# SiLU written as tanh in a two-layer kernel: activation in the exponentials' table, product on VectorE

## The chip, the cores and the metric

The kernel runs on one core of a Trainium2 chip. The metric is the device time of one execution in microseconds (us); a time given for a kernel is the median of several executions. The engines are called as the profile calls them: PE (TensorE, matrix multiplications), PEld (PE's weight loads), DVE (VectorE), ACT (ScalarE, activations), POOL (GpSimd) and SP (the queue that issues most DMAs). PSUM is the memory that PE writes to, in eight banks; SBUF is the working memory.

## The reference, cut to what matters

Two layers, each a gated residual: `x = x + s * g`, where `s` comes from one branch and `g = silu(f)` from another, both computed from the layer-normalised `x` (2 sequences of 2048 tokens, 256 channels).

```python
x = L0_attn_x
xn = _layernorm(x, axis=-1)
s = _L0_attn_ref(xn, ...)          # linear attention (elu features), then @ W_out
g = _silu(_L0_ffn_ref(xn, ...))    # softmax attention block, then a mixture of 8 experts
x = x + s * g
xn = _layernorm(x, axis=-1)
s = _L1_attn_ref(xn, ...)          # causal softmax attention, 16 heads, then @ Wo
g = _silu(_L1_ffn_ref(xn, ...))    # one quantised linear map plus a low-rank one
x = x + s * g
```

`silu(v) = v / (1 + exp(-v))`, which is the same as `0.5 * v * (1 + tanh(v / 2))`.

## The kernel before, in words

Tokens lie in 32 tiles of 128 (16 per sequence); `xr` holds all of them in SBUF. The work has three stages, one after the other.

1. **Layer 0's attentions** (from 0 to about 1440 us). The softmax attention of the expert branch, with the linear branch `s` worked in between. The linear branch's result is copied from PSUM by ACT (line 1199) and stored to the DRAM tensor `s_dram`.
2. **The experts** (to about 1931 us). Two halves of eight experts; for each, PE multiplies by W1 (L1380), ACT applies Gelu (L1381), PE multiplies by W2 (L1386), DVE adds the bias (L1389). Within it `early_mix` finishes layer 0 for the first four tiles: POOL gathers the expert rows (L1337), DVE weighs and adds them (L1344 to L1346), ACT applies Silu (L1348), DVE multiplies by `s` and adds `x` (L1349, L1350).
3. **Layer 1's attention** (to the end). Per sequence and group of four heads, pass A finds each query's maximum (PE L554, DVE L573 or, on the diagonal, L567), pass B computes scores again (PE L587, L1585, L520), ACT takes the exponentials into `pt` (L599), POOL adds up pairs of key tiles in `ps` (L1597 to L1602), PE multiplies by the values and sums (L1620, L1631), DVE collects (L1635, L1637), and `finish` projects with `wo` (PE L1676), multiplies by the gate (DVE L1680) and adds to `xr` (POOL L1686).

Between these run two side jobs of stage 3 that contain a SiLU:

- **`mix`** finishes layer 0 for the other 28 tiles, two tiles (one buffer pair `gx`, `xs`; there are two of each) at a time: four gathers by POOL (L1459), weighing by ACT (L1468), two additions by DVE (L1473, L1474), Silu by ACT (L1439), then times `s` and plus `x` (L1481, L1482), on DVE for the first sequence and on POOL for the second, and the statistics of the next layer norm (L491 on) for every four tiles. For the second sequence `mix` is called with four tiles: both pairs' Silus are then one step, so that they are together. Those four calls come at units 24, 40, 56 and 72 of the attention's loop.
- **`gate`** computes layer 1's `g` for four tiles: PE L1698, L1713, L1714 into two PSUM banks, then one ACT step with both Silus (L1720), which reads PSUM and writes `gs`, then DMAs to the DRAM tensor `g_dram`; `finish` loads it again.

Stages 1 and 3 are ordered by hand: every piece of work is a step `S(strand, engine, cost, function, reads, writes)`, and `Plan.run` searches, with these costs in us, for the order in which steps are issued; each engine then executes its steps strictly in that order. A changed cost or step can therefore change the order of everything after it. Stage 2 is ordered by the Tile scheduler.

ACT evaluates its functions from a table that must be loaded (ACT_TABLE_LOAD in the profile). Exp, Gelu and Silu are loaded separately here; the compiler puts a load wherever the next function is not in the table that is there.

## Time and profile before

| | us |
|---|---|
| five runs | 3439.91, 3442.41, 3443.70, 3433.20, 3444.74 |
| median | 3442.41 |
| the profiled execution, its own time | 3440.51 |
| the profiled execution, span from first to last instruction | 3438.7 |
| PE busy | 3317.3 (96%) |
| DVE busy | 2077.0 (60%) |
| ACT busy | 1669.3 (49%) |
| POOL busy | 1664.5 (48%) |

A page or an answer of the trace names a group of instructions by the line of the kernel, the engine, the operation, what it writes and reads, how often it ran, its busy time and the mean of one; then the time that the engine sat idle just before and who released it. "PE banks L1631 <- POOL ps L1602" reads: PE's instruction of line 1631 waited for POOL's of line 1602. Time in a window counts from the first instruction.

### The profile page before, as it was taken

Reading aid. Unit: us, or ns where it says so; the run is one execution under the profiler, and the core shown is the slowest. Engines: PE = TensorE matmul, PEld = TensorE weight load, DVE = VectorE, ACT = ScalarE, POOL = GpSimd, SP = SyncE. Lnnn points to the kernel's source line nnn. Section 1 sums busy time; section 2 is a strip of 40 time slices with the busy share of each in tenths; the row PEclk is TensorE's granted clock in tenths of the full one; section 3 lists DMA queues with packets and bytes.
Section 4 is the critical chain, followed back from the end, with each engine's and each line's share of the span. In section 5 each row is a group of like instructions: output and inputs, shape, how many; then the busy total and the mean of one; then the engine's idle time right before and its main releaser. Section 6 shows DMA issues by size and latency. Waiting matters only on the chain.

```text
span 3438.7 us, 84330 instructions
## 1 busy us (share of the span) xinstructions
PE 3317.3 (96%) x35894; PEld 2327.5 (68%) x35894; DVE 2077.0 (60%) x4066; ACT 1669.3 (49%) x3330; POOL 1664.5 (48%) x2239
## 2 busy tenths in 40 slices
PE   6999999999999999799899999999999999999998
PEld 5667777776777777566566566666676666766675
DVE  4767676777676768511111377676666566666674
ACT  3565555555555555411221364555455545454554
POOL 5452322324232223300100268898786567787876
PEclk7999999999999999899999999999999999999999
DMA  5000000000000010233333211110000100000000
GB/s 182 2 2 2 8 8 8 17 20 32 8 8 5 8 39 25 96 106 108 117 115 97 69 49 50 52 49 12 17 16 26 38 28 14 22 14 19 14 26 23
DMA packets 99514, 133.21 MB, mean 39 GB/s; under 512 B 9395, under 2 KB 76671, under 8 KB 99138
## 3 DMA queue, kind: packets, MB, share of 16 engines
q1 hardware_dynamic: 92994, 113.95, 10.3%
q0 software_dynamic: 6144, 13.88, 1.3%
q8 instruction: 281, 4.60, 0.5%
q14 instruction: 95, 0.78, 0.1%
HBM read 92.96 MB, written 37.75 MB: 38 GB/s over the span
## 4 chain that ended last, share of the span: by engine, by line
PE 78%; POOL 12%; DVE 4%; issue 3%; ACT 2%; DMA 1%; SPq 0%; POOLq 0%; DVEq 0%; ACTq 0%
PE banks L554 14%; PE banks L587 13%; PE banks L838 7%; PE s L1386 6%; PE s L1380 6%; PE banks L1620 5%; PE banks L520 4%; PE banks L1527 3%; POOL ps L1601 3%; PE banks L768 3%; POOL ps L1602 2%; POOL ps L1597 2%; PE banks L1585 2%; DVE mx L573 2%; PE banks L1100 2%
## 5 line engine op out<-in xcount | busy, mean ns | idle before, releaser
L599 ACT ACTIVATE pt<-banks 128x512 f32<-128x512 f32 (+1 forms) x2304 | 1164.0, 575 | 712.2 <-PE banks L520 209.3
L573 DVE TENSOR_REDUCE mx<-banks 128x2 f32<-128x1024 f32 (+3 forms) x1024 | 1120.9, 1122 | 336.2 <-PE banks L587 140.0
L554 PE MATMUL banks<-carried,carried 32*128 32x512 f32 (+3 forms) x5120 | 1233.2, 559 | 13.4 <-DVE mx L573 6.1
L587 PE MATMUL banks<-carried,carried 32*128 32x256 f32 (+1 forms) x9216 | 1237.0, 387 | 2.1 <-DVE mx L573 1.6
L587 PEld LDWEIGHTS banks<-carried,carried 32*128 32x128 f32 x9216 | 924.0, 185 | 35.0 <-DVE mx L573 5.2
L554 PEld LDWEIGHTS banks<-carried,carried 32*128 32x128 f32 x5120 | 482.6, 185 | 208.2 <-issue 112.8
L1597 POOL TENSOR_TENSOR ps<-pt 128x1024 f32<-128x1024 f32 (+1 forms) x159 | 343.2, 2158 | 144.4 <-ACT pt L599 118.3
L1601 POOL TENSOR_TENSOR ps<-ps,pt 128x1024 f32<-128x1024 f32 x127 | 300.8, 2369 | 68.2 <-ACT pt L599 63.7
L775 POOL TENSOR_TENSOR ra<-raw,rope 128x128 f32<-128x128 f32 x128 | 60.2, 470 | 557.5 <-ACT raw L787 479.9
L1585 PE MATMUL banks<-mh,ones_h 3*128 3x512 bf16 (+1 forms) x1152 | 292.3, 368 | 0.1
L567 DVE CUSTOM_DVE_ANT_0 banks<-banks,causal 128x384 f32<-128x384 f32 (+3 forms) x512 | 242.1, 513 | 58.4 <-PE banks L554 50.9
L1620 PE MATMUL banks<-pt,vt 128*32 128x256 f32 (+1 forms) x4608 | 270.8, 373 | 2.7 <-ACT pt L599 2.6
L1602 POOL TENSOR_TENSOR ps<-ps,pt 128x1024 f32<-128x1024 f32 (+1 forms) x127 | 267.9, 2109 | 10.0
L838 PE MATMUL banks<-pt,vt 128*32 128x256 f32 (+1 forms) x4608 | 268.2, 371 | 2.0 <-DVE mx L573 1.4
L1389 DVE TENSOR_TENSOR ye<-s,b 128x256 f32<-128x256 f32 x64 | 27.2, 425 | 386.3 <-PE s L1386 386.3
L1381 ACT ACTIVATE hm<-s,b1c 128x512 f32<-128x512 f32 x128 | 87.8, 687 | 351.9 <-PE s L1380 351.9
L1386 PE MATMUL s<-carried,hm 128*128 128x256 f32 x1024 | 226.6, 382 | 7.7 <-ACT hm L1381 7.7
L1380 PE MATMUL s<-xt,carried 128*128 128x512 f32 x512 | 225.9, 599 | 7.1 <-DVE xt L1322 7.0
L1620 PEld LDWEIGHTS banks<-pt,vt 128*32 128x32 f32 x4608 | 134.2, 110 | 140.7 <-ACT pt L599 42.0
L1386 PEld LDWEIGHTS s<-carried,hm 128*128 128x128 f32 x1024 | 196.4, 192 | 42.1 <-ACT hm L1381 8.1
L520 PEld LDWEIGHTS <-ident_h 32*128 32x128 bf16 x4096 | 201.5, 93 | 30.7 <-issue 15.4
L838 PEld LDWEIGHTS banks<-pt,vt 128*32 128x32 f32 x4608 | 133.3, 109 | 117.3 <-issue 14.9
(273 smaller groups left out, 4165.4 us busy)
## 6 DMA issues: line engine op xcount, KB each, us to landing
carried<-in_L_ffn_W_dram SPq DMA_DIRECT2D x32, 1024.0 KB, 5.9
gl<-g_dram SPq DMA_DIRECT2D x64, 256.0 KB, 2.8
slots_in<-zero SPq DMA_DIRECT2D x8, 1024.0 KB, 11.1
xe<-slots_in SPq DMA_DIRECT2D x16, 512.0 KB, 7.6
slots_out<-ye SPq DMA_DIRECT2D x16, 512.0 KB, 6.9
s_dram<-lo SPq DMA_DIRECT2D x16, 256.0 KB, 2.0
hn<-in_L_attn_x_dram SPq DMA_DIRECT2D x16, 256.0 KB, 2.8
g_dram<-gs SPq DMA_DIRECT2D x16, 256.0 KB, 2.2
```

The costliest lines, as they stand in the source:

```text
L520: nc.tensor.matmul(out, ident_h[r, q], mask[r, q], start=False, stop=q == 3)
L554: nc.tensor.matmul(s.t[:, x, :w], g.qt.t[r, t * P : (t + 1) * P], g.kt.t[r, 512 * k : 512 * k + w], start=True, stop=not (diagonal and cau ...
L573: S("A", "DVE", t_dve(2 * w), lambda: nc.vector.tensor_reduce(mx.t[:, t % 2, i : i + 2, k], s.t[:, :, :w], AX.X, ALU.max), r=[(s, 0), (s, ...
L587: nc.tensor.matmul(s.t[:, at], g.kt.t[r, kj * P : (kj + 1) * P], g.qt.t[r, QC * c + q0 : QC * (c + 1)], start=n == 0, stop=n == 1 and not ...
L599: S("B", "ACT", t_act(w), lambda: nc.scalar.activation(pt.t[:, j, :w], s.t[:, :w], AF.Exp, scale=0.25), r=[s], w=[(pt, j)])
L838: nc.tensor.matmul(av.t[32 * j : 32 * j + 32, q0:QC], vts[G.vn][:, kj, j], pt.t[:, j, at], start=n == 0, stop=n == len(tiles) - 1,)
L1380: nc.tensor.matmul(ps, w1[:, k, f * P : (f + 1) * P], xt[:, k], start=k == 0, stop=k == 1)
L1386: nc.tensor.matmul(ps[:, :D], hm[:, f, s * P : (s + 1) * P], w2[:, f], start=f == 0, stop=f == FF // P - 1)
L1585: return lambda: nc.tensor.matmul(s.t[:, :w_], ones_h[r], G.mh[c].t[r, 512 - w_ :], start=False, stop=last)
L1597: nc.gpsimd.tensor_tensor(ps.t[:, :, q0:], pt.t[:, :, same], pt.t[:, :, odd], ALU.add)
L1601: nc.gpsimd.tensor_tensor(ps.t, ps.t, pt.t[:, :, even], ALU.add)
L1620: nc.tensor.matmul(av.t[32 * j : 32 * j + 32, q0:QC], G.vt.t[:, kj, j], pt.t[:, j, at], start=n == 0, stop=False)
```

## The change

Silu is replaced by Tanh with the input scaled by 0.5, followed by one `scalar_tensor_tensor` on DVE that computes `(tanh + 1) * v`. The result is twice the SiLU, so a factor of 0.5 is put elsewhere: in layer 0 on the linear branch's result when it is copied from PSUM, in layer 1 on the output weights `wo`, once, by POOL. With that, `gate`'s step for two Silus becomes four steps (one Tanh and one product for each pair), the step costs given to the planner change, and the second sequence's `mix` is called eight times with two tiles (at units 24, 32, ..., 80) instead of four times with four.

```diff
-            S("lin", "ACT", 0.59, lambda: nc.scalar.copy(so.t.rearrange("p n d -> p (n d)"), sp.t), r=[sp], w=[so])
+            S("lin", "ACT", 0.59, lambda: nc.scalar.mul(so.t.rearrange("p n d -> p (n d)"), sp.t, 0.5), r=[sp], w=[so])
...
-            nc.scalar.activation(gx[:, 0], gx[:, 0], AF.Silu)
+            nc.scalar.activation(gx[:, 1], gx[:, 0], AF.Tanh, scale=0.5)
+            nc.vector.scalar_tensor_tensor(gx[:, 0], gx[:, 1], 1.0, gx[:, 0], ALU.add, ALU.mult)
...
                     load_l1()
+                    nc.gpsimd.tensor_scalar_mul(wo, wo, 0.5)
...
-                    nc.scalar.activation(gx.t[:, 0], gx.t[:, 0], AF.Silu)
+                    nc.scalar.activation(gx.t[:, 1], gx.t[:, 0], AF.Tanh, scale=0.5)
...
-            S("mix", "ACT", 1.4 + 0.6 * len(both), silus, r=got, w=got)
+            S("mix", "ACT", 0.6 * len(both), silus, r=got, w=got)
...
+            S("mix", "DVE", 1.0, lambda: nc.vector.scalar_tensor_tensor(
+                gx.t[:, 0], gx.t[:, 1], 1.0, gx.t[:, 0], ALU.add, ALU.mult
+            ), r=[gx], w=[gx])
...
-            def silu():
-                for py, gl in pairs:
-                    nc.scalar.activation(gl.t.rearrange("p n d -> p (n d)"), py.t, AF.Silu)
-
-            S("gate", "ACT", 4.0, silu, r=[py for py, _ in pairs], w=[gl for _, gl in pairs])
+            def silu(py, gl):
+                nc.scalar.activation(gl.t.rearrange("p n d -> p (n d)"), py.t, AF.Tanh, scale=0.5)
+
+            def times(py, gl):
+                g_ = gl.t.rearrange("p n d -> p (n d)")
+                nc.vector.scalar_tensor_tensor(g_, g_, 1.0, py.t, ALU.add, ALU.mult)
+
+            for py, gl in pairs:
+                S("gate", "ACT", 0.6, lambda py=py, gl=gl: silu(py, gl), r=[py], w=[gl])
+                S("gate", "DVE", 0.7, lambda py=py, gl=gl: times(py, gl), r=[py, gl], w=[gl])
...
-        others = [(24 + 16 * n, lambda n0=NT + 4 * n: mix(n0, 4)) for n in range(NT // 4)]
+        others = [(24 + 8 * n, lambda n0=NT + 2 * n: mix(n0)) for n in range(NT // 2)]
```

## The prediction

> **What bounds the kernel now.** I read the page first: the table of engines, the slices, the chain.

> ```profile
> PE 3317.3 (96%) x35894; PEld 2327.5 (68%) x35894; DVE 2077.0 (60%) x4066; ACT 1669.3 (49%) x3330; POOL 1664.5 (48%) x2239
> ...
> PE   6999999999999999799899999999999999999998
> ...
> POOL 5452322324232223300100268898786567787876
> PE 78%; POOL 12%; DVE 4%; issue 3%; ACT 2%; DMA 1%; SPq 0%; POOLq 0%; DVEq 0%; ACTq 0%
> ```

> PE sets the end: it is busy in every slice but the first and two near the experts, and it holds 78% of the chain that ended last. ACT holds 2% of that chain, though it is busy for 49% of the span. So a microsecond taken from ACT is worth one only where PE was waiting for it. POOL holds 12%, and is at eight to nine tenths in slices 24 to 27, which is where the second sequence's `mix` runs.

> Next the groups of ACT's instructions, for what the change takes away:

> ```profile
> L599 ACT ACT_TABLE_LOAD x15 | 19.2, 1283 | 2.8 <-PE banks L1714 1.4 <-PE banks L1585 1.2
> ...
> L1439 ACT ACT_TABLE_LOAD x9 | 11.5, 1283 | 0.2
> ...
> L1720 ACT ACT_TABLE_LOAD x6 | 7.7, 1283 | 0.1
> ...
> L1348 ACT ACT_TABLE_LOAD x1 | 1.3, 1283 | 0.0
> ```

> Thirty loads of 1283 ns lie in stage 3, from 1942.9 to 2788.5 us: 38.5 us of ACT. Then who held PE up in stage 3 (window 1930 to 3439, the waits of PE alone; who waited for whom, total, times, longest):

> ```profile
> PE banks L1631 <- POOL ps L1602: 11.6, 10, 2.4
> PE banks L1571 <- POOL mpad L1567: 6.5, 14, 1.6
> PE banks L554 <- DVE mx L573: 2.8, 14, 0.4
> PE banks L1620 <- ACT pt L599: 2.6, 7, 1.3
> PE banks L372 <- ACT hn L1501: 2.3, 4, 1.2
> ```

> All waits for ACT in that answer add up to 10.5 us (2.6 for `pt` and 2.3 for `hn` above; 1.4, 1.2, 1.1, 1.1 and 0.8 in rows not shown), those for POOL to 18.4 (11.6, 6.5, 0.3), those for DVE to 8.7. In 1500 us, ACT costs PE 10.5 us whatever it does. That is the ceiling for the direct gain, not 38.5.

> **The change part by part.** The sum starts from the profiled execution's 3440.5 us, 1.9 below the median of the five runs (3442.4); I add the 1.9 at the end.

> *Loads.* In the changed program as built, ACT's order has 3 loads instead of 34: Exp at the start, Gelu at the experts, Exp at layer 1. Tanh needs none of its own, beside Gelu either. Two terms follow.

> (a) The early Silu, among the experts. Here the timeline shows ACT on the path:

> ```profile
> 1711.99 1.28 ACT L1381 ACT_TABLE_LOAD   x1
> ...
> 1713.29 0.69 ACT L1381 ACTIVATE hm<-s,b1c 128x512 f32<-128x512 f32 x1
> ...
> 1714.03 12.48 PE L1386 MATMUL s<-carried,hm 128*128 128x256 f32 x44 [7.67 <-ACT hm L1381]
> ```

> PE stood 7.67 us, because ACT, in its order, waited for the gathered rows of `early_g` before it could do the last Gelu. The load before the Silu (1701.07) lies inside that wait of 8.57 us and is worth nothing; the load after it is in the path: **-1.3 us**. The new product on DVE (128x1024; the neighbouring L1349 took 1.22) comes after Tanh and delays only early_mix's own end, and the bias addition L1389 by under 0.5 us, which PE's other banks cover. The wait of 7.67 stays otherwise: the place in the order is the same, after 71 Gelus.

> (b) Stage 3. I went through PE's stops after each load: 0.68 us at 1964.8 (`xt` behind a load and three exponentials), 0.53 at 1976.1, 0.44 at 2002.9, 0.64 at 2099.5, 1.32 at 2633.8, each with a load just ahead of the `pt` or `xt` that PE waited for. Sum 3.6: **-3.6 us**. The other 25 loads are hidden by PE's own work, as ACT idles 362.6 us before L599 in stage 3. Bounds: 0 (something else is late next) to -10.5 (all waits for ACT).

> [...]

> (c) *Smaller portions of `mix`.* Total work on POOL stays (32 gathers, 16 operations of 1.27 us for the second sequence), but it comes in eight portions instead of four. One call of four tiles gives POOL 8 gathers of 1.0 with 0.3 between them and 4 operations, some 15 us at once, while its sums for the attention (L1597 to L1602, 2.4 us each for a full tile) go on. From 2080 to 2360, PE's waits for POOL are 9.5 us (5.7 for `ps` L1602, 3.5 for `mpad`, 0.3). With half portions the backlog halves, the average load of POOL (89% there) does not. Between 0 and -9.5 I take a third: **-3.0 us**.

> (d) *The new product of `mix` on DVE.* 14 instructions, 6 for the first sequence and 8 for the second, each reading two operands from SBUF. The undisturbed price is that of the same form in L1084, 680 to 694 ns. But the rows that stand right beside it say more:

> ```profile
> L1473 DVE TENSOR_TENSOR gx<-gx,xr x14: 674/692/3500, 1941.7 to 2321.4; 128x512 f32<-128x512 f32 x14
> ```

> ```profile
> 2081.03 3.50 DVE L1473 TENSOR_TENSOR gx<-gx,xr 128x512 f32<-128x512 f32 x1
> ```

> At the same time POOL ran a gather and then the 2.36 us of L1597; DVE's instruction ended after POOL's. For the 16 executions of L1473 and L1474 from 2080 to 2360 the means are 1.61 and 1.39 us, 0.81 above 0.69. So the eight new ones bring 8 x 0.81 = 6.5 us of stall on DVE beside 14 x 0.69 = 9.7 of work. DVE's reduction L573 frees the banks into which PE writes; it is 64 to 77% busy in the stretches there. In the stretch after the 3.50 us PE stopped 1.05 us for L573, so a stall is passed on in part. Between 0 and +6.5 I take half: **+3.3 us**. POOL pays too: its additions took 2.69 to 2.82 instead of 2.36 us when they met these; that is within (c)'s bounds.

> [...]

> (e) *The product of `gate`.* 16 instructions that read one operand from PSUM. L1680 has that shape and takes 673 to 690 ns in all 64 executions, never more, so 11 us on a DVE that is 58% busy from 2600 to 2800. It holds a PSUM bank for 0.7 us longer, plus DVE's queue; on the other hand ACT no longer waits between the two Silus in one step (20.7 us of idle time before L1720 for PE), so exponentials can go between. Between -1.5 and +3: **+0.5 us**.

> (f) *Nothing:* L1199 as a multiplication costs what L1154 does, 597 instead of 585 ns, 16 times, on an ACT that waits for PE there; stage 1's order is unchanged. The scaling of `wo` is one POOL operation of 128x1024, about twice L1599's 0.64 us, placed where POOL then idles 242 us. The stores of `g` (SP) come one by one, and are needed tens of us later. In the start of stage 3 (1931 to 2080) the chain from gather to projection loses loads and gains a product of 0.7 for each pair; in the new order the second pair's Tanh stands behind the first gate's, so I count no gain beyond (b) there.

> Sum: -1.3 - 3.6 - 3.0 + 3.3 + 0.5 = **-4.1**. 3440.5 - 4.1 = 3436.4, with the 1.9: **3438.3 us**.

> **The rivals.**

> *Forecast* (51%): the loads were mostly hidden, and POOL and DVE trade. 3438, within 3435.5 and 3449.3, which is 0.2% on either side of the median and about what a measurement of this kernel can tell from no change.

> *Faster* (35%): POOL's backlog, not its load, made PE's stops, and ACT's stops all go: -1.3 - 8.5 (of 10.5) - 6 (of 9.5) + 2 = -13.8, 3428.6. For it: POOL's 12% of the chain, and stops of 2.36, 1.56 and 1.33 us all in the mixes of four tiles. Against it: POOL's load, 89% on average there, does not fall.

> *Slower* (14%): the products meet POOL's additions at their worst, on DVE in stage 3's second sequence. Seven of the 16 neighbours took over 1.5 us, mean 2.5, which is 1.8 above the undisturbed one. If the eight new ones all do, and PE pays in full: +14.7, less the 4.9 of (a) and (b): +9.8, 3452. It decides once the eight stall for over 12 us together, 1.5 us each.

> *No effect beyond (a):* 3441; it lies inside the forecast.

> **How the numbers follow.** The likeliest case gives 3438. The range reaches over most of both others: 3426 to 3449. Faster by over 0.2%: 0.35; within: 0.51; slower: 0.14.

> **What would show it.** Three loads in all, ACT some 37 us less busy in stage 3; PE's stop among the experts 6.4 instead of 7.67; in stage 3 PE's waits for ACT 7 us instead of 10.5, for POOL 15 instead of 18.4; DVE's new product at 0.69 us for the first sequence, about 1.5 for the second, and 0.69 for the gate. Wrong would be: waits for POOL near zero (then (c) was too small), or the product over 2.2 us (then (d)). A different order of the whole of stage 3, which the planner is free to choose, can add or take a few us that none of these steps names.

## The result and the profile after

| | us |
|---|---|
| before, median of 53 runs beside it | 3442.0 |
| after, median of 30 runs | 3447.6 (3440.5 to 3454.3) |
| ratio after to before, 95% interval | 1.0018 [1.0012, 1.0023] |
| forecast | 3438 (3426 to 3449) |
| the profiled execution of after, its own time | 3447.95 |
| its span | 3446.0 |

The time is about 6 us above the kernel before, where some 4 below were forecast. It lies inside the range, on the other side of the old time.

From the page of the kernel after, the lines that answer to those shown of before:

```profile
PE 3312.1 (96%) x35894; PEld 2325.9 (67%) x35894; DVE 2103.9 (61%) x4097; ACT 1629.2 (47%) x3299; POOL 1670.1 (48%) x2240
...
PE   6999999999999999799899999899999999999998
...
POOL 5452232325232223300100258899876667877877
...
PE 75%; POOL 14%; DVE 4%; issue 3%; ACT 2%; DMA 1%; POOLq 0%; SPq 0%; DVEq 0%; ACTq 0%
```

ACT lost 40 us of work, as forecast, and PE's busy time is 5 us less. PE stood for 133.9 us (span less busy time) instead of 121.4, and the mean granted clock is 0.982 in both profiled executions: over the whole execution it is PE's standing that grew, not its time at a lower clock. Another slice of PE, the 26th (2154 to 2240 us), fell to 8, where POOL stands at 8 to 9 tenths in five slices running, and POOL's part of the chain went from 12 to 14%.

The groups of ACT's table loads (busy time, mean ns):

```profile
L727 ACT ACT_TABLE_LOAD x1 | 1.3, 1283 | 10.2 <-DVE ln_st L491 10.2
...
L1386 ACT ACT_TABLE_LOAD x1 | 1.3, 1283 | 17.1 <-DMA xe<-slots_in 17.1
...
L599 ACT ACT_TABLE_LOAD x1 | 1.3, 1283 | 0.0
```

Three are left of 34. The waits of PE in stage 3 (total, times, longest), to be read against the five lines of before:

```profile
PE banks L1579 <- POOL mpad L1575: 17.6, 19, 2.6
PE banks L1639 <- POOL ps L1610: 12.4, 8, 3.0
PE banks L554 <- DVE mx L573: 3.0, 13, 0.8
PE banks L1667 <- ACT rw L1673: 2.9, 3, 1.7
PE banks L372 <- ACT hn L1509: 2.3, 4, 1.2
```

L1579 and L1575 are before's L1571 and L1567, L1639 and L1610 its L1631 and L1602. PE's waits for POOL are 32.0 us instead of 18.4; those for ACT and DVE hardly moved (9.7 after 10.5, 8.3 after 8.7). By stages, up to the first product with W1, through the experts, and from there, before took 1452.9, 477.7 and 1508.1 us, after 1450.8, 477.1 and 1518.1. So the loss is all in stage 3, and within it in one stretch, shown by the windows of before and of after (us, then busy time of PE, PEld, DVE, ACT, POOL, then granted clock, DMA share, GB/s):

```profile
2080.00:2440.00 360.00, 345.88 (x3985) 237.70 (x3978) 246.91 (x490) 194.59 (x376) 316.42 (x287) 0.99 0.11 34
```

```profile
2080.00:2440.00 360.00, 333.91 (x3943) 228.13 (x3939) 252.88 (x498) 176.80 (x358) 322.84 (x293) 0.98 0.12 36
```

PE is idle 26.1 us there instead of 14.1. This is the second sequence's `mix`.

The two new products, as groups of DVE in after:

```profile
L1486 DVE SCALAR_TENSOR_TENSOR gx<-gx 128x512 f32<-128x512 f32 x14 | 12.2, 869 | 1.1 <-ACT gx L1444 0.9
...
L1731 DVE SCALAR_TENSOR_TENSOR gs<-gs,banks 128x512 f32<-128x512 f32 x16 | 10.8, 678 | 21.3 <-ACT gs L1727 21.3
```

Both are as cheap as forecast or cheaper in themselves. But DVE stood 21.3 us in its queue at the gate's product, waiting for Tanh; the prediction named no such stand.

### The profile page after: what moved, and what is told of

Same layout as the page of the kernel before. It is cut to its first block, busy times and chain, and to the rows that moved or that the text cites. A ratio compares the mean times of both kernels' runs of the same rounds, so it can differ in the third digit from the quotient of the medians.

```text
span 3446.0 us, 84355 instructions
## 1 busy us (share of the span) xinstructions
PE 3312.1 (96%) x35894; PEld 2325.9 (67%) x35894; DVE 2103.9 (61%) x4097; ACT 1629.2 (47%) x3299; POOL 1670.1 (48%) x2240
## 4 chain that ended last, share of the span: by engine, by line
PE 75%; POOL 14%; DVE 4%; issue 3%; ACT 2%; DMA 1%; POOLq 0%; SPq 0%; DVEq 0%; ACTq 0%
PE banks L554 14%; PE banks L587 12%; PE banks L838 7%; PE s L1391 6%; PE s L1385 6%; PE banks L1628 5%; PE banks L520 3%; POOL ps L1609 3%; PE banks L768 3%; POOL ps L1610 3%; PE banks L1535 2%; POOL ps L1605 2%; PE banks L1593 2%; PE banks L1100 2%; DVE mx L573 2%
## 5 line engine op out<-in xcount | busy, mean ns | idle before, releaser
L599 ACT ACTIVATE pt<-banks 128x512 f32<-128x512 f32 (+1 forms) x2304 | 1163.7, 575 | 724.9 <-PE banks L1593 216.0
L573 DVE TENSOR_REDUCE mx<-banks 128x2 f32<-128x1024 f32 (+3 forms) x1024 | 1120.9, 1122 | 325.3 <-PE banks L587 143.9
L554 PE MATMUL banks<-carried,carried 32*128 32x512 f32 (+3 forms) x5120 | 1233.6, 561 | 12.3 <-DVE mx L573 6.3
L554 PEld LDWEIGHTS banks<-carried,carried 32*128 32x128 f32 x5120 | 483.3, 185 | 204.4 <-issue 109.4
L1610 POOL TENSOR_TENSOR ps<-ps,pt 128x1024 f32<-128x1024 f32 (+1 forms) x127 | 268.8, 2116 | 10.0
L1386 ACT ACTIVATE hm<-s,b1c 128x512 f32<-128x512 f32 x128 | 87.9, 687 | 350.3 <-PE s L1385 350.3
L838 PEld LDWEIGHTS banks<-pt,vt 128*32 128x32 f32 x4608 | 133.3, 109 | 117.3 <-issue 14.9
```

The costliest lines, as they stand in the source:

```text
L554: nc.tensor.matmul(s.t[:, x, :w], g.qt.t[r, t * P : (t + 1) * P], g.kt.t[r, 512 * k : 512 * k + w], start=True, stop=not (diagonal and cau ...
L573: S("A", "DVE", t_dve(2 * w), lambda: nc.vector.tensor_reduce(mx.t[:, t % 2, i : i + 2, k], s.t[:, :, :w], AX.X, ALU.max), r=[(s, 0), (s, ...
L599: S("B", "ACT", t_act(w), lambda: nc.scalar.activation(pt.t[:, j, :w], s.t[:, :w], AF.Exp, scale=0.25), r=[s], w=[(pt, j)])
L838: nc.tensor.matmul(av.t[32 * j : 32 * j + 32, q0:QC], vts[G.vn][:, kj, j], pt.t[:, j, at], start=n == 0, stop=n == len(tiles) - 1,)
L1610: nc.gpsimd.tensor_tensor(ps.t[:, :, q0:], ps.t[:, :, q0:], pt.t[:, :, odd], ALU.add)
```

## The experiments

Three things could be at fault: the products on DVE (in their work, "P", or because DVE stands at them, "W"), the planner's new order ("O"), which every changed step draws anew, or the split of `mix` into smaller portions. The five groups ran on five chips. On those of the first and second group before had a lower granted clock (0.975 on average, 0.981 on the others), so a time is compared only through its ratio to before in the same group; that even a ratio need not carry over is shown by the fifth group. A ratio need not be the quotient of the two medians to the last digit (e1's medians give 0.9978, its ratio is 0.9971).

### First group: before 3495.8 us

**e1, Tanh alone**, in before's order, with no product and no factor of a half (the multiplication by x is left out):

```diff
-            nc.scalar.activation(gx[:, 0], gx[:, 0], AF.Silu)
+            nc.scalar.activation(gx[:, 0], gx[:, 0], AF.Tanh, scale=0.5)
```

and the same at the other two places.

> The kernel before with Tanh in place of each Silu and nothing else (the products by x and the factors of a half are left out, so the output is another); every engine's order is that of before, less 31 table loads. It prices the loads alone. Theory O (the new order and the eight portions of mix cost, by putting POOL's work for the attention late): 4 to 6 us faster than before, about 3437, from the early load (1.3) and PE's stops behind loads (3.6). Rival P (the new products on DVE cost): the same, 4 to 6 us faster. Rival N (loads are hidden wholly, something else is late in their place): 0 to 2 us faster.

Measured: 3488.0 us, 0.9971 [0.9960, 0.9982]. Without the loads this chip gained 0.3%, some 10 us, about twice what was expected.

**e2, after without `mix`'s product**, in after's order (the step stays in the plan and issues nothing; the factor is left out):

```diff
-            S("mix", "DVE", 1.0, lambda: nc.vector.scalar_tensor_tensor(
-                gx.t[:, 0], gx.t[:, 1], 1.0, gx.t[:, 0], ALU.add, ALU.mult
-            ), r=[gx], w=[gx])
+            S("mix", "DVE", 1.0, lambda: None, r=[gx], w=[gx])
```

> The changed kernel, in its own order on every engine, without the 14 products of mix on DVE (the step stays and issues nothing; the output is another). Theory O: 0 to 2 us faster than the changed kernel, so still 4 to 6 us slower than before, about 3447. Rival P: the cost goes, 3442 or less.

Measured: 3500.4 us, 1.0015 [1.0001, 1.0028]. After without these products is no nearer to before than after itself.

**e3, after with portions of four**, as before had them:

```diff
-        others = [(24 + 8 * n, lambda n0=NT + 2 * n: mix(n0)) for n in range(NT // 2)]
+        others = [(24 + 16 * n, lambda n0=NT + 4 * n: mix(n0, 4)) for n in range(NT // 4)]
```

> The changed kernel with the second sequence's mix called four times with four tiles, as before (units 24, 40, 56, 72). Theory O, if the portions are what puts POOL late: PE's waits for POOL in stage 3 return from 32 to some 18 to 20 us, the time to 3436 to 3441. If it is the order as such and not the portions, anything between 3436 and 3452. Rival P: no better than the changed kernel, about 3447 or more.

Measured: 3516.3 us, 1.0055 [1.0042, 1.0067]. Undoing the split alone makes it worse, so the split is not what costs here; but this is another order once more. PE's waits for POOL did fall, to 15.4 us, lower than O expected, and the time rose all the same: these waits do not stand for the time.

**e7, the whole change in before's order**, each product issued in the same step as its Tanh, so that the planner does not see it:

```diff
-                    nc.scalar.activation(gx.t[:, 0], gx.t[:, 0], AF.Silu)
+                    nc.scalar.activation(gx.t[:, 1], gx.t[:, 0], AF.Tanh, scale=0.5)
+                    nc.vector.scalar_tensor_tensor(gx.t[:, 0], gx.t[:, 1], 1.0, gx.t[:, 0], ALU.add, ALU.mult)
```

> The whole computation of the change in the order of before: each product is issued on DVE inside ACT's step right after its Tanh, unseen by the planner; mix of four, both gates in one step. Theory O: the gain of the loads less a little for DVE, 1 to 5 us faster than before, 3437 to 3441. Rival P: slower than before by 4 us or more, 3446 or above.

Measured: 3514.2 us, 1.0056 [1.0043, 1.0069]. Against e1 the same order with the products is 0.85% slower by the two ratios (0.75% by the medians). So products can cost much; whether by their work or by their place was open.

### Second group: before 3492.1 us

**r1, after again.**

> The changed kernel itself, unaltered, as the mark for the other runs of this chip. Theory P (the 30 products on VectorE cost more time in stage 3 than the 31 table loads gave) and theory O (the planner's new order is at fault, POOL's backlog above all) both expect 1.001 to 1.004 of the kernel before, and PE's waits for POOL in stage 3 again near 32 us.

Measured: 3497.1 us, 1.0011 [0.9998, 1.0024]. The ratio held; PE's waits for POOL did not: 18.3 us here, with 14.9 for DVE. On this chip, at a mean clock of 0.975, the same order met other waits than in after's profiled execution at 0.982, where POOL's were 32.0.

**r2 and r3, other draws.** The planner tries handicaps from a random generator; here only its start is changed, in after (r2) and in before (r3):

```diff
-        draw = random.Random(0)
+        draw = random.Random(self.SEED)
...
+        plan.SEED = 1
```

(the second line for layer 1's plan alone; layer 0's keeps 0).

> The changed kernel with another start of the planner's random draws: the same work, portions and products, in another order. Theory O: another order can lose the backlog on POOL, so the ratio to the kernel before moves by 0.3% or more against the unaltered changed kernel, or falls below 1.000. Theory P: the ratio stays within 0.2% of the unaltered changed kernel's, above 1.000.

> The kernel before with another start of the planner's random draws: nothing of the change. Theory O: orders differ by 0.2 to 0.5% (7 to 17 us) with no change of the work, so this kernel lies outside 0.998 to 1.002. Theory P says nothing firm; if the order hardly matters it is within 0.1% of the kernel before.

Measured: r2 3495.8 us, 1.0009 [0.9999, 1.0019]; r3 3513.7 us, 1.0058 [1.0042, 1.0073]. r2 lies within 0.2% of r1, as P expected. r3 is outside 0.998 to 1.002, as O expected: before, with nothing changed but the draw, loses three times what the change lost or more.

**r4, before with the split alone**, Silu and its loads kept:

```diff
-        others = [(24 + 16 * n, lambda n0=NT + 4 * n: mix(n0, 4)) for n in range(NT // 4)]
+        others = [(24 + 8 * n, lambda n0=NT + 2 * n: mix(n0)) for n in range(NT // 2)]
```

> The kernel before with only the split: the mix of the second sequence in eight portions of two tiles at 24+8n instead of four portions of four, Silu and its table loads kept (so up to eight more loads of about 1.3 us on ACT). Theory O, if the split is what brings the backlog: 1.003 to 1.008 of the kernel before, and PE's waits for POOL well above 18.4 us. Theory P: the split costs at most its loads, 0.999 to 1.003, with POOL's waits near 18 us.

Measured: 3504.3 us, 1.0028 [1.0014, 1.0041], PE's waits for POOL 17.9 us. The waits are P's, not O's. The time is at the end of P's range and, by its interval, reaches into O's: the loads that the split adds, and one more order, cannot be told apart here.

### Third group: before 3441.2 us

**r5, products placed later.** As e7, but a product is put on a list and issued after three more DVE steps, or earlier if a step needs its result, its buffer or its bank:

```diff
-                    nc.vector.scalar_tensor_tensor(gx.t[:, 0], gx.t[:, 1], 1.0, gx.t[:, 0], ALU.add, ALU.mult)
+                    plan.defer(lambda g=gx.t: nc.vector.scalar_tensor_tensor(g[:, 0], g[:, 1], 1.0, g[:, 0], ALU.add, ALU.mult), [gx])
...
+            self.settle(lambda x: x[0] + 3 <= self.count)
```

> Tanh and all 30 products in the order of the kernel before, as in the run with the products in the old order (1.0056), but each product is issued up to three steps later in VectorE's queue (at the latest right before what reads its result or takes its bank), so that VectorE seldom stands in it waiting for Tanh. Theory W (VectorE's stand in its queue at the product, waiting for Tanh, and the clock that is halved after each stop of PE, are what cost): PE's waits for DVE in stage 3 fall from 23 to some 10 us, the time to 0.997 to 1.001 of the kernel before, near the run with Tanh alone. Theory P (the products' work itself, 30 of about 0.7 to 1 us on VectorE, beside POOL): it stays at 1.004 or above.

Measured: 3446.0 us, 1.0013 [1.0003, 1.0023]. The same 30 products, one to six instructions later in DVE's queue, cost 0.4% less than in e7: most of that cost belongs to their place, not to their work. It missed W's range by a little; PE's waits for DVE fell from 23.3 us in e7 to 14.1, where 10 were expected. That W's stand is the way in which the place costs is not shown by this run, as the traces of r14 below will say.

**r6, after without any product**, order and all else kept (the factor is left out for `mix` and `gate`):

```diff
-                S("gate", "DVE", 0.7, lambda py=py, gl=gl: times(py, gl), r=[py, gl], w=[gl])
+                S("gate", "DVE", 0.7, lambda: None, r=[py, gl], w=[gl])
```

on top of e2's edit.

> The changed kernel's order with none of the 30 products (mix and gate leave out the factor: what Tanh gives is multiplied on, so the output is not the reference's); portions, places and factors of a half stay. Theory O (the order that the planner draws for the change is a worse one, apart from the products): 1.000 to 1.002 of the kernel before, as the changed kernel. Theory P or W (the products, by work or by waits): 0.996 to 0.998, as Tanh alone in the old order.

Measured: 3437.9 us, 0.9994 [0.9986, 1.0003]; between the two ranges. PE still waits 26 us for POOL in this order. The first lines of PE's waits in stage 3:

```profile
PE banks L1577 <- POOL mpad L1573: 13.9, 19, 2.0
PE banks L1637 <- POOL ps L1608: 10.5, 7, 3.0
PE banks L554 <- DVE mx L573: 3.5, 14, 0.8
```

So most of the growth from 18.4 us belongs to the order; the products put some 6 us on top (one trace of each). But the kernel with these 26 us of waits is no slower than before: its stage 3 took 1507.6 us in the profiled execution, before's 1508.1.

**r7 and r8, a third draw** (start 2) for after and for before.

> The changed kernel with a third start of the planner's random draws. Theory O (orders differ by more than the change is worth): the ratio to the kernel before is anywhere in 0.997 to 1.008, and differs from the unaltered changed kernel's by over 0.2% as likely as not. Theory P: 1.000 to 1.003.

> The kernel before with a third start of the planner's random draws, nothing of the change in it. Theory O: above 1.002 again, as with the second start (1.0058): the order of the kernel before is then a good draw among such orders, and any new order loses some 0.2 to 0.6% whatever it is for. If it lies at 1.000 or below, the second start's 1.0058 was a bad draw and the first is an ordinary one.

Measured: after 3458.7 us, 1.0060 [1.0044, 1.0075]; before 3466.7 us, 1.0079 [1.0064, 1.0094]. With r2 and r3 that makes three orders of each kernel: before 1, 1.0058 and 1.0079, after 1.0011, 1.0009 and 1.0060. Before's own order is the best of its three by 20 us.

### Fourth group: before 3441.6 us

Variants of r5, to find what its products still cost.

**r9, products spread**: for the second sequence in halves, with two DVE steps between; POOL's multiply and add follow.

```diff
+                    for t in range(2) if n0 >= NT else (slice(None),):
+                        plan.defer(lambda g=gx.t, t=t: nc.vector.scalar_tensor_tensor(
+                            g[:, 0, t], g[:, 1, t], 1.0, g[:, 0, t], ALU.add, ALU.mult
+                        ), [gx], by=3 if n0 < NT else 2 + 4 * n + 2 * t)
```

> The full change in the order of before with the products placed later (1.0013), and the products of the second sequence's mix cut in halves of 128x256, with two other VectorE steps between the halves; POOL's multiply and add follow them. Theory Q (pairs of products with both operands in SBUF hold VectorE for 2 to 4 us while POOL runs, the row maxima behind them come late, PE stops and its clock is halved for 7 to 14 us): the stops near the four portions shrink, 0.997 to 1.000. Theory G (the gate's products or VectorE's load in general): 1.001 to 1.002, unchanged.

Measured: 3448.1 us, 1.0019 [1.0007, 1.0032]. No gain: Q missed.

**r10, without the second sequence's products** (`if n0 < NT:` ahead of `plan.defer`), and **r11, without the gate's** (that `plan.defer` left out).

> The products placed later in the order of before, but without the eight of the second sequence's mix (the factor is left out there, so the output is not the reference's). Theory Q: 0.997 to 0.999 of the kernel before. Theory G: 1.000 to 1.0015.

> The products placed later in the order of before, but without the gate's sixteen (left out, so the output is not the reference's); the fourteen of mix stay. Theory Q: 1.0005 to 1.0015, as with them. Theory G: 0.997 to 0.999.

Measured: r10 3445.3 us, 1.0010 [1.0001, 1.0019]; r11 3444.9 us, 1.0010 [0.9997, 1.0023]. Neither group alone is worth anything that can be told from r5's 1.0013. r10 contradicts Q and r11 contradicts G, so neither says what is left.

**r12, Silu kept in the second sequence's `mix`**, Tanh elsewhere:

```diff
+                    if n0 >= NT:
+                        nc.scalar.activation(gx.t[:, 0], gx.t[:, 0], AF.Silu)
+                        continue
```

> As the products placed later in the order of before, but the mix of the second sequence keeps Silu, four portions with two table loads each, and has no product (s is halved for the first sequence alone); the output is the reference's. Theory Q: the loads there cost less than the products, 0.997 to 0.9995 of the kernel before. Theory G: 1.000 to 1.002.

Measured: 3442.3 us, 1.0002 [0.9991, 1.0014]. With the whole computation it is level with before, no better; that is in G's range.

### Fifth group: before 3440.2 us

e1 and e7 once more, on a chip with the clock of the first comparison.

> Tanh for Silu in the order of before, no products and no factors, as in the first experiment (0.9971 there, on a chip with a lower clock). If the loads are worth that on any chip: 0.996 to 0.998, and the products placed later cost 0.4% together, though either group alone seems to cost nothing. If the gain belongs to the other chip: 0.9985 to 1.000, and the products placed later cost 0.1 to 0.2%.

> All products right behind Tanh in the order of before, as in the fourth experiment (1.0056 there). If VectorE's stand at the products is what costs, on any chip: 1.003 to 1.007, well above the products placed later (1.0013). If it belongs to the other chip: 1.001 to 1.002, no different from placing them later.

Measured: r13 (Tanh alone) 3441.4 us, 1.0001 [0.9989, 1.0012]; r14 (products right behind Tanh) 3459.5 us, 1.0059 [1.0042, 1.0076]. The cost of the place repeats. The 0.3% that the loads were worth does not: it belongs to the other chip. No kernel with the whole computation beat before.

### What r13's and r14's traces show

PE's waits in stage 3 of r13, Tanh alone:

```profile
PE banks L1631 <- POOL ps L1602: 11.8, 10, 2.4
PE banks L1571 <- POOL mpad L1567: 6.2, 15, 1.6
PE banks L554 <- ACT gx L1439: 3.7, 1, 3.7
PE banks L554 <- DVE mx L573: 2.9, 15, 0.4
PE banks L1527 <- ACT xt L1508: 2.6, 2, 1.9
```

POOL's two lines are before's, to 0.3 us. Four of the five stops that term (b) of the prediction counted went: 0.53 us at 1976, 0.44 at 2003, 0.64 at 2100 and 1.32 at 2634 have no counterpart. The fifth, 0.68 us at 1964.8, stayed, and grew to 1.94:

```profile
1959.75 1.28 ACT L599 ACT_TABLE_LOAD   x1
...
1961.04 1.25 ACT L599 ACTIVATE pt<-banks 128x384 f32<-128x384 f32 x3
...
1962.17 0.61 ACT L1508 COPY xt<-banks 128x512 f32<-128x512 f32 x1
...
1962.83 1.16 PE L1527 MATMUL banks<-xt,wg 128*128 128x512 f32 x1 [1.94 <-ACT xt L1508]
```

The load ahead of it is the one of the first exponentials of layer 1, which the change keeps. The third line of the waits is no new stop either. In before the same products of L554 wait at the same place, under another name. What they need is DVE's copy of `carried`, which ended at 1940.08 in r13, and ACT's Tanh, named there, ended at 1940.15:

```profile
PE banks L554 <- DVE carried L1534: 2.1, 1, 2.1
```

That copy stands in DVE's queue behind the adding of gathered rows that ACT weighs, and for those ACT waited 4.95 us of DMA in r13 and 4.92 in before. PE went on 9.2 us after the start of its L1527 in both (1940.23 less 1931.08, and 1943.94 less 1934.70). It only came to the stop sooner in r13: the eight products of L1527 took 3.70 us there, and 5.33 in before, where the granted clock was 0.50 from 1934.6 to 1938.0. So the two stops grew by 2.8 us together, as much as the other four gave (2.9). What PE gains ahead of a stop that another chain ends, it loses at that stop.

In r14 the product groups of DVE:

```profile
L1725 DVE SCALAR_TENSOR_TENSOR gs<-gs,banks 128x512 f32<-128x512 f32 x16 | 10.8, 685 | 28.0 <-ACT gs L1724 28.0
...
L1442 DVE SCALAR_TENSOR_TENSOR gx<-gx 128x512 f32<-128x512 f32 x14 | 24.0, 1738 | 2.7 <-ACT gx L1441 2.7
```

The idle time ahead of the first line is what theory W names: DVE stands 28.0 us for the gate's Tanh, with its row maxima queued behind. In r5 that is 0. The second line is another thing: `mix`'s product takes 1738 ns on average where after's order gave 869, and r5's place 1122. So r5 changed both, and no run separates them; r2, which stands 23.8 us at the gate's product, is at 1.0009, so the stand alone does not decide. The timeline of r14 shows how the second line comes about:

```profile
2183.19 2.81 POOL L1600 TENSOR_TENSOR ps<-pt 128x1024 f32<-128x1024 f32 x1
...
2184.91 1.64 DVE L1477 TENSOR_TENSOR gx<-gx 128x512 f32<-128x512 f32 x1
2186.07 2.69 POOL L1604 TENSOR_TENSOR ps<-ps,pt 128x1024 f32<-128x1024 f32 x1
2186.47 5.58 DVE L1442 SCALAR_TENSOR_TENSOR gx<-gx 128x512 f32<-128x512 f32 x2
...
2188.84 2.67 POOL L1605 TENSOR_TENSOR ps<-ps,pt 128x1024 f32<-128x1024 f32 x1
...
2191.98 1.21 DVE L573 TENSOR_REDUCE mx<-banks 128x2 f32<-128x1024 f32 x1
...
2193.24 0.79 PE L554 MATMUL banks<-carried,carried 32*128 32x128 f32 x2 [5.15 <-DVE mx L573]
```

DVE's line is two products, of 2.84 and 2.82 us, each begun beside a running POOL addition and each ended 0.55 us after that addition did; undisturbed they would take 0.68, as the shortest of the group does. The row maximum behind them comes 4.2 us late, and PE stands for 5.15 us.

What this stop of PE cost beyond itself is in the granted clock. The same stretch of r14 in windows:

```profile
2176.00:2186.00 10.00, 10.00 (x113) 7.22 (x109) 9.11 (x19) 8.29 (x17) 9.84 (x4) 1.00 0.08 26
2186.00:2192.00 6.00, 2.09 (x16) 0.84 (x14) 6.00 (x4) 2.19 (x4) 5.85 (x3) 0.99 0.00 0
2192.00:2199.00 7.00, 5.76 (x39) 4.75 (x41) 3.75 (x12) 1.80 (x4) 3.78 (x8) 0.52 0.00 0
2199.00:2209.00 10.00, 10.00 (x142) 7.36 (x140) 7.62 (x22) 5.87 (x12) 9.70 (x9) 1.00 0.01 2
```

After the stop PE has half its clock for 7 us (0.52 on average), and then all of it (1.00). Over the runs of the fifth group, the span times one minus the mean granted clock is 64.9 us for before and 84.7 for r14: +19.8, where the span rose by 20.1. By this measure the net loss of r14 is as large as its added time at half clock. The products' own share is read better against r13, which has the same order and the same three loads: 15.1 of 20.0 us. The rest is PE standing: 127.8 us in the profiled execution of r14, 121.6 in that of r13. The measure is an upper bound, as it also counts the half clock while PE stands.

For r13 the same sum says 69.6 us: 4.7 more than before, with an equal span. The rest of the span is 4.7 us shorter, which is about what the prediction wanted of the loads, as if the clock had taken it back. The clock of a run is recorded to 0.001 (3.4 us), so this is a hint from averages over 12 and 17 runs, not a proof.

## Why the prediction missed

In time, two steps failed, and they are of like size. The loads, (a) and (b), were to give 4.9 us, and in r13 they gave nothing that can be told from zero. The products, (d) and (e), were to cost 3.8, and from r6 to after it is 8. A third step, (c), had PE's waits for POOL wrong by a factor of two, but what that cost in time is not shown.

**(a) The load in the early SiLU, -1.3: fits.** In r13, PE goes on after its stop 259.8 us after the experts' start, in before 261.1 (1709.96 less 1450.2, and 1714.03 less 1452.9). Single traces scatter by as much: the four with Silu there give 259.7 to 261.3, the sixteen with Tanh 258.1 to 260.3. But their means, 260.5 and 259.1, differ by 1.4 us. The sign that was named for it failed: the stop itself was to fall from 7.67 to 6.4 us, and it took 7.44 in r13 and 7.88 in after, because PE also arrived earlier at it.

**(b) PE's stops behind loads, -3.6: four of the five stops went, the time did not.** With the order fixed, r13 stands at 1.0001, -3.8 to +4.1 us, where (a) and (b) together wanted -4.9. The step counted 0.68 us behind a load that the change keeps (in after's own order that load comes behind the copy `xt` and holds nothing up), and took the rest, 2.9 us, as time that PE would not lose elsewhere. In r13's trace two other stops grew by 2.8 us, at places where a DMA or the load that stays sets the time. The step's own lower bound, "something else is late next", is what happened. On the chip with the lower clock the same edit was worth 0.3%, so this term depends on the chip.

**(c) Smaller portions of `mix`, -3.0: wrong about PE's waits; its worth in time is open.** The forecast said that PE would wait 15 us for POOL; it waited 32.0. The step reasoned from before's stops as if the rest of the order stood still. It does not: r6, after's order with no product in it, has PE waiting 26 us for POOL. But the waits are not the time. r6 is at 0.9994 and r13, in before's order with 18.3 us of these waits, at 1.0001, so the new order and the split together show no cost, as far as two chips of like clock can be compared; e3 and r14, with 15.4 and 12.4 us, are among the slow ones. Whether the split itself costs stays open: r4 (split alone) lost 0.28%, e3 (split alone undone) lost 0.55%, more than after, and each of them is also a new draw. (POOL's slices at eight to nine tenths, put at 24 to 27, are the 25th to the 28th.)

**(d) `mix`'s product, +3.3: the stall too large for after's order.** Fourteen at 869 ns make 12.2 us, 2.5 above 14 times 0.69, where 6.5 of stall were feared. The second sequence's eight averaged 1.0 us, not 1.5. That the product stalls beside POOL's additions was right (in r14 two of them ended 0.55 us after the addition beside which they began), and dear in another order: in r14 the second sequence's eight took 2.10 us each, 11.3 us of stall together, close to the 12 at which the "Slower" rival was to decide, and r14 is 20 us slower. But that is another place of the products, not the one that after's order has. One reading was off: L1084's form, put at 680 to 694 ns, reaches 880.

**(e) The gate's product, +0.5: the instruction right (678 ns), the queue missed.** DVE stands 21.3 us at it in after. The step spoke of "DVE's queue" only as something that holds a bank longer; that DVE's own next work stands behind a wait for ACT was not priced. r5 against r14 shows that places of the products cost up to 0.45% together. What the 21.3 us cost in after is not shown: PE's waits for DVE did not rise there, and no run took the gate's products alone out of after's order.

**(f) Nothing: right** as far as the runs reach; stage 1 took 1450.8 us after 1452.9.

**The sum.** Its gains, (a) to (c), were -7.9; r6, which has them all, is at -0.06%, -2 us [-4.8, +1.0]. Its costs, (d) and (e), were +3.8; from r6 to after it is +0.24% or 8 us, 5 to 12 by the two intervals. The two were not run side by side, and r13 beside e1 shows that chips can differ by 0.3%. So too much was counted as gain and, as far as the two comparisons can be put together, too little as cost. Which of the two kinds of product makes the 8 us is open: e2, without `mix`'s, was no nearer to before, which points at the gate's, but on a chip of the other kind.

**What was wrong above the terms.** "A different order of the whole of stage 3 ... can add or take a few us that none of these steps names" stands at the end of the prediction as an afterthought. It can be the largest term. Three draws of one kernel spread over 27 us (0.79%), more than six times the whole forecast gain, and before's is the best of its three. The draw that the change got shows no cost by itself (r6 beside r13), but what the same products cost depends on their place: about 4 us in r5, 8 in after, 20 in r14, the first and the last against r13. With three orders of each kernel it can't be said that the change is worse in itself.

## What to carry to other kernels

Where a planner or a scheduler redraws the order, first measure how far orders of the unchanged work differ, by another start of its search; a change of less than that is judged by keeping the order fixed, as r13 and r14 do. A new instruction costs its place in the queue before it costs its duration (in after DVE stood 21.3 us at the gate's products, whose work is 10.8): ask what its engine does while it waits, and what is queued behind. Do not add up TensorE's waits as if they were the time: with 44 us of them in stage 3 r6 was level with before, which has 38, and with 42 r14 was 20 us slower. A stop of TensorE can cost more than its length: the one of 5.15 us in r14 was followed by 7 us at a granted clock of 0.52.

## What the runs showed of the hardware

```profile
2081.40:2084.80 3.40, 3.40 (x26) 1.70 (x20) 3.30 (x2) 2.70 (x6) 3.23 (x3) 1.00 0.22 68
2084.80:2088.20 3.40, 2.35 (x21) 1.52 (x19) 3.34 (x8) 0.68 (x2) 3.07 (x3) 1.00 0.28 77
2088.20:2091.60 3.40, 3.40 (x27) 3.17 (x27) 0.82 (x5) 1.72 (x4) 3.32 (x3) 0.50 0.00 0
2091.60:2095.00 3.40, 3.40 (x58) 1.88 (x52) 3.29 (x4) 3.39 (x8) 2.16 (x1) 1.00 0.02 5
```

PE was busy for 2.35 of 3.40 us, and the next step ran at half clock (0.50), which by estimate, half of 3.4, costs up to 1.7 us more than the stop. So a stop of a third of a step was followed by it. As far as the profile shows, the length of the stop alone does not decide, and theory W of r5, with the clock halved after each stop, went too far. Later in the same trace PE stood for 1.56 us of a step, and the clock stayed:

```profile
2337.40:2340.80 3.40, 1.84 (x36) 0.86 (x32) 1.24 (x9) 0.01 (x1) 3.32 (x3) 1.00 0.02 5
2340.80:2344.20 3.40, 3.23 (x22) 1.40 (x16) 1.92 (x6) 0.43 (x1) 3.05 (x8) 1.00 0.00 0
```

What else decides is not known from these runs.

**Chips differ.** Before took 3440 to 3442 us at a mean clock of 0.981 in the last three groups and 3492 to 3496 at 0.975 in the first two; most of it is in stage 1, 1483 to 1493 us in the traces of the first two groups and 1445 to 1453 in the others, for nearly the same instructions. Why is not known. A term measured on one (Tanh alone, 0.9971) need not hold on the other (1.0001).

**`mix`'s product on DVE ended after the POOL addition beside which it began.** In r14 the two products from 2186.47 us on each began while a POOL addition ran (2.69 and 2.67 us) and ended 0.55 us after it: 5.58 us for two, where the shortest of that sequence's eight took 0.68 and the median 2.64. In after the one at 2140.64 us began beside an addition of 2.81 us, ended 0.56 us after it and took 1.71.
